# Two 3x3 convolutions on one core: bands of 16 rows on the whole array, or of 8 rows on its quarters

## The chip, the cores and the metric

The kernel runs on one core of a Trainium2 chip. The core has five engines that run side by side and wait for each other through semaphores: TensorE (PE in the profile; its weight loads are PEld), VectorE (DVE), ScalarE (ACT), GpSimd (POOL) and SyncE (SP, which only issues transfers here). 16 DMA engines move data between the large memory (HBM) and the on-chip memory (SBUF), which has 128 partitions. Matrix products land in PSUM, a small memory of eight banks of 512 f32 values per partition. The metric is the device time of one execution in microseconds.

## The reference, cut to what matters

The input is 4 images of 8 channels, 512 x 512, f32. Four layers follow each other, each of the form x = x + f(groupnorm(x)), with 4 groups of 2 channels per image:

```python
x = x + _L0_conv_ref(_gn(x), ...)      # a spiking attention block, 512 x 512 matrices
x = x + _L1_conv_ref(_gn(x), w)        # depthwise 13 x 13, reflected edges
x = x + _L2_conv_ref(_gn(x), w2, b2)   # 3 x 3, 8 to 8 channels, x and w rounded to [-127, 127]
x = x + _L3_conv_ref(_gn(x), w3, b3)   # 3 x 3, 8 to 8 channels, f32
```

Layer 2's rounding scale is 127 / max|groupnorm(x)| over all four images, so nothing of layer 2 can start before layer 1 has ended everywhere. Layer 3's group norm of one image needs layer 2 of that whole image.

## The kernel before, in words

One program, written for a scheduler: the source gives the instructions of each engine, the scheduler sets their order per engine by data dependences and by the buffers of each pool, and every engine then runs its own list strictly in that order. A tile pool with `bufs=n` gives a tag n buffers; the next user of a buffer waits for the last reader of it.

*Layer 0* (`layer0`, the first 2,124 us) and the sums for layer 1's norm (`st1`) are not touched.

*Layer 1* (`layer1`): per group of two channels g, channel b and image t, the whole channel is loaded (two transfers on SP's queue, L667), a banded weight `bt` with norm and residual in it is formed on DVE (L675), and for each of four parts eight f32 products (L684) run: 112 partitions in, 64 out, two halves `q` of the image in the two column halves of the array. ACT evicts (L691), DVE takes statistics (`bn_stats`, L694) and, once per channel and image, the maximum and minimum over 2,048 values (L696, L697). The result goes to HBM (`x2d`, L700, ACT's queue). All four groups' layer 1 norms (`group_stats`, L149 to L167) are computed as layer 1 starts.

*Layers 2 and 3* (`layers23`) hold the image in 37 windows: 16 rows x 8 channels = 128 partitions, stepping by 14 rows. A 3 x 3 convolution is three banded products, one per horizontal tap `dx`, with a 128 x 128 weight that holds the vertical taps (`banded`). Within a row the pixels are kept in four phases (every fourth pixel together); `conv` (L810) needs five products per window, since a neighbour in the outer phases lies in another phase. After layer 1 the weights are built (L740, L744), the norm and the scale for the rounding computed (L753 to L794, with an all-reduce over partitions on POOL), and then five rounds run:

```python
for ks in groups:                      # 12 groups of 3 windows, and one of 1
    if t < T: layer2(t, x3, st3, ks)
    if before is not None:
        for k in ks: layer3(t - 1, before[0], m3, r3, k)
if t < T: halos(x3)
```

Per group `layer2` loads three windows (L827, SP), subtracts and scales on DVE (L834), clips on POOL (L838), rounds to bf16 on DVE (L841), runs the products, and per window evicts with the residual on DVE (L848), adds the bias on ACT (L851) and takes statistics (L852). Per window `layer3` norms on DVE (L865), runs f32 products, evicts with bias and residual on DVE in pixel order (L873) and stores (L879, POOL's queue). `halos` (L857 to L860) copies the rows that windows share from window to window, once per image, as two large transfers and a small one on SP's queue. x3 has two whole-image buffers.

Of the kernel before, what the change touches and what calls it, by code (L numbers as in the profile page):

```python
# [33 lines left out]
F32 = mybir.dt.float32  # L34
# [28 lines left out]
W2_ROWS, W2_STEP, W2_N = 16, 14, 37  # L63
W2_START = [W2_STEP * k for k in range(W2_N - 1)] + [N - W2_ROWS]
W2_VALID = [(0, 15)] + [(1, 15)] * (W2_N - 2) + [(9, 16)]
# [5 lines left out]
def shape_constants():  # L71
# [3 lines left out]
    mask2 = np.zeros((W2_ROWS, B, W2_N, 2), np.float32)  # L75
    for k, (a, b) in enumerate(W2_VALID):
        mask2[a:b, :, k] = 1
# [17 lines left out]
    c24 = np.zeros((3, B, 2 * W2_ROWS - 1, B), np.float32)  # L95
    for dy in range(3):
        c24[dy, np.arange(B), W2_ROWS - 2 + dy, np.arange(B)] = 1
# [4 lines left out]
def network(ctx: ExitStack, tc: tile.TileContext, i: dict, out: bass.AP):  # L102
# [74 lines left out]
    hi = late.tile([P, T, B], F32, name="hi")  # L177
    lo = late.tile([P, T, B], F32, name="lo")
    with ExitStack() as s:
        layer1(  # L180
            s, tc, i, x1d, x2d, avg_quarter, group_stats, st1, st2, hi, lo, band1d
        )
    with ExitStack() as s:
        layers23(s, tc, i, x2d, out, ind, mask2, avg, avg_same, group_stats, st2, hi, lo)
# [436 lines left out]
def layer1(s, tc, i, x1d, x2d, avg, group_stats, st1, st2, hi, lo, band1d):  # L621
    nc = tc.nc
    ps_c = s.enter_context(tc.tile_pool(name="ps_c", bufs=4, space=PSUM))
    ps_1 = s.enter_context(tc.tile_pool(name="ps_2", bufs=1, space=PSUM))
# [25 lines left out]
    for g in range(G):  # L650
        m, r = group_stats(
            st1[g].rearrange("p t b c k (h z) -> p t (b c k h) z", z=3), T, PAIR * NC * 4, None,
            avg, ps_1, f"x1_{g}", n_each=D // 4,
        )
        mr = bp.tile([P, T], F32, tag="mr", name=f"mr_{g}")
        nc.vector.tensor_mul(mr, m, r)
        for b in range(g * PAIR, (g + 1) * PAIR):
# [4 lines left out]
            for t in range(T):  # L662
# [16 lines left out]
                for a in range(n_half // N_PS1):  # L679
# [13 lines left out]
                    )  # L693
                    nc.vector.bn_stats(st2[:, t, b, a, :], xo[:, a, :])  # L694
                flat = xo.rearrange("p a n -> p (a n)")
                nc.vector.tensor_reduce(hi[:, t, b : b + 1], flat, AX.X, ALU.max)  # L696
                nc.vector.tensor_reduce(lo[:, t, b : b + 1], flat, AX.X, ALU.min)  # L697
# [11 lines left out]


def layers23(
    s, tc, i, x2d, out, ind, mask2, avg, avg_same, group_stats, st2, hi, lo
):
    nc = tc.nc
    ps_2 = s.enter_context(tc.tile_pool(name="ps_q", bufs=3, space=PSUM))
    ps_3 = s.enter_context(tc.tile_pool(name="ps_r", bufs=3, space=PSUM))
    ps_1 = s.enter_context(tc.tile_pool(name="ps_3", bufs=1, space=PSUM))
    wpool = s.enter_context(tc.tile_pool(name="w2", bufs=1))

    def col(name, n=1):  # L720
        return wpool.tile([P, n], F32, name=name)

    n_taps = 3 * B
    c24 = wpool.tile([n_taps, i["c24"].shape[1]], F32, name="c24")
    nc.scalar.dma_start(c24, i["c24"])
    w2 = wpool.tile([n_taps, n_taps], F32, name="w2t")
    nc.scalar.dma_start(w2, i["w2"])
    w3 = wpool.tile([n_taps, n_taps], F32, name="w3t")
    nc.scalar.dma_start(w3, i["w3"])
    b2, b3 = col("b2"), col("b3")  # L730
    nc.scalar.dma_start(b2, i["b2"])
    nc.scalar.dma_start(b3, i["b3"])

    def banded(w, dtype, name):

        band = wpool.tile([P, 3, P], dtype, name=name)
        ps = ps_1.tile([P, W2_ROWS, n_taps], F32, tag="misc", name=f"ps_{name}")
        for row in range(W2_ROWS):
            at = (W2_ROWS - 1 - row) * B
            nc.tensor.matmul(  # L740
                ps[:, row, :], lhsT=c24[:, at : at + P], rhs=w, start=True, stop=True
            )
        for dx in range(3):
            nc.vector.tensor_copy(  # L744
                band[:, dx, :].rearrange("p (r c) -> p r c", c=B), ps[:, :, dx * B : (dx + 1) * B]
            )
        return band

    band3 = banded(w3, F32, "band3")


    wall = wpool.tile([P, n_taps * n_taps], F32, name="wall")
# [186 lines left out]
```

## Time and profile before

| what | us |
|---|---|
| runs shown | 3325.26, 3325.86, 3328.9; median 3325.86 |
| the profiled execution | 3325.98, of which the span from first to last instruction 3324.2 |
| layer 1, first to last product | 2129.6 to 2583.8 |
| first product of layer 2 | 2622.6 |
| PE busy | 3086.2 (93%) |
| DVE busy | 2433.7 (73%) |
| POOL busy | 886.1 (27%) |
| ACT busy | 368.8 (11%) |

In the profile's lists a row names line, engine, operation, output <- inputs by the program's names, the shapes, a count, then busy time, the mean of one in ns, and the idle time before it with what ended it. An f32 product is recorded as two passes. A row of a table of windows gives a stretch of the span, busy time of PE, PEld, DVE, ACT and POOL with the number of instructions, the clock that PE was granted as a share of full speed, the busy share of the 16 DMA engines and the GB/s moved. The chain lists, in order of time, what each step waited for, back from the last instruction. All times of instructions are from the start of the span.

### The profile page before, as it was taken

Reading aid. Unit: us, or ns where it says so; the run is one execution under the profiler, and the core shown is the slowest. Engines: PE = TensorE matmul, PEld = TensorE weight load, DVE = VectorE, ACT = ScalarE, POOL = GpSimd, SP = SyncE. Lnnn points to the kernel's source line nnn. Section 1 sums busy time; section 2 is a strip of 40 time slices with the busy share of each in tenths; the row PEclk is TensorE's granted clock in tenths of the full one; section 3 lists DMA queues with packets and bytes.
Section 4 is the critical chain, followed back from the end, with each engine's and each line's share of the span. In section 5 each row is a group of like instructions: output and inputs, shape, how many; then the busy total and the mean of one; then the engine's idle time right before and its main releaser. Section 6 shows DMA issues by size and latency. Waiting matters only on the chain. (4 is left out here: it accounts for less than half of the span.)

```text
span 3324.2 us, 35901 instructions
## 1 busy us (share of the span) xinstructions
PE 3086.2 (93%) x13090; PEld 1633.4 (49%) x13090; DVE 2433.7 (73%) x3751; ACT 368.8 (11%) x545; POOL 886.1 (27%) x1874
## 2 busy tenths in 40 slices
PE   8999999999999999999999999899999449696979
PEld 6555555555555555555555555433334325454545
DVE  5997787797797797788688688555555569696955
ACT  1300000000000000000000000021111121111100
POOL 1332341341342242243243233100000113232322
PEclk9999999999999999999999999899999669898989
DMA  4222212222122221221111111588777245454533
GB/s 169 80 83 65 65 65 77 65 65 73 62 64 71 65 67 63 77 65 64 52 46 55 55 43 40 131 213 213 199 204 204 57 96 137 107 136 101 134 80 84
DMA packets 284406, 315.02 MB, mean 95 GB/s; under 512 B 17424, under 2 KB 197784, under 8 KB 283877
## 3 DMA queue, kind: packets, MB, share of 16 engines
q1 hardware_dynamic: 191040, 200.86, 22.8%
q0 software_dynamic: 22128, 68.09, 6.5%
q10 hardware_dynamic: 71061, 43.78, 4.4%
q8 instruction: 102, 1.67, 0.2%
q14 instruction: 75, 0.61, 0.1%
HBM read 204.84 MB, written 103.17 MB: 93 GB/s over the span
## 5 line engine op out<-in xcount | busy, mean ns | idle before, releaser
L398 PE MATMUL ps_in<-w_v,xn 128*128 128x512 f32 x1024 | 460.1, 598 | 2.5 <-issue 2.2
L810 PE MATMUL ps_conv<-xn,band 128*128 128x128 f32 (+2 forms) x1480 | 415.9, 439 | 46.6 <-DVE xn L865 46.6
L684 PE MATMUL ps_conv<-x,bt 112*64 112x512 f32 x2048 | 448.6, 595 | 4.6 <-issue 3.4
L398 PE MATMUL ps_in<-w_k,xn 128*128 128x512 f32 x1024 | 450.3, 593 | 1.0 <-DVE v_k L363 0.7
L398 PE MATMUL ps_in<-xn,w_q 128*128 128x512 f32 x1024 | 449.6, 592 | 0.2
L434 PE MATMUL ps_b<-toep,vtok 128*64 128x512 bf16 x3072 | 371.8, 382 | 0.0
L810 PEld LDWEIGHTS ps_conv<-xn,band 128*128 128x128 f32 x1480 | 246.5, 196 | 210.0 <-issue 89.0
L684 PEld LDWEIGHTS ps_conv<-x,bt 112*64 112x64 f32 x2048 | 175.3, 135 | 274.6 <-issue 273.4
L461 PE MATMUL ps_out<-wp,so 128*128 128x512 f32 x1024 | 309.0, 444 | 0.0
L483 POOL COPY x1s<-x1s 128x2 f32<-128x2 f32 (+1 forms) x1024 | 226.2, 274 | 297.1 <-DVE x1s L472 297.1
L398 PEld LDWEIGHTS ps_in<-w_k,xn 128*128 128x128 f32 x1024 | 194.1, 190 | 222.4 <-issue 206.2
L398 PEld LDWEIGHTS ps_in<-xn,w_q 128*128 128x128 f32 x1024 | 191.9, 190 | 219.9 <-issue 213.3
L371 POOL TENSOR_TENSOR h_v<-h_v,c_v 128x512 f32<-128x512 f32 x96 | 122.9, 1281 | 656.5 <-DVE h_v L370 622.0
L398 PEld LDWEIGHTS ps_in<-w_v,xn 128*128 128x128 f32 x1024 | 190.3, 190 | 219.1 <-issue 213.6
L434 PEld LDWEIGHTS <-vtok 128*64 128x64 bf16 x3072 | 209.3, 111 | 124.3 <-issue 3.8
L873 DVE SCALAR_TENSOR_TENSOR o<-ps_conv,b,x 128x512 f32<-128x512 f32 x148 | 167.6, 1140 | 123.7 <-PE ps_conv L810 74.5
L346 ACT ACTIVATE h_q<-v_q,c_half 128x512 f32<-128x512 f32 x96 | 69.3, 722 | 1542.6 <-DVE v_q L342 1542.6
L461 PEld LDWEIGHTS ps_out<-wp,so 128*128 128x128 f32 x1024 | 192.7, 188 | 94.1 <-issue 59.0
L167 POOL TENSOR_TENSOR grstd_x<-grstd_x,neg_half 128x1 f32<-128x1 f32 (+2 forms) x25 | 19.4, 775 | 811.3 <-DVE grstd_x L166 679.7
L472 DVE SCALAR_TENSOR_TENSOR x1s<-v_p,xr 128x256 f32<-128x256 f32 x256 | 186.0, 766 | 17.5 <-DMA x<-x1s 5.9
L694 DVE BATCH_NORM_STATS2 st<-xo 128x6 f32<-128x512 f32 x128 | 88.5, 691 | 148.1 <-ACT xo L691 148.1
L810 PE MATMUL ps_conv<-xq,band 128*128 128x128 bf16 (+2 forms) x740 | 119.5, 318 | 68.6 <-DVE xq L841 67.4
(149 smaller groups left out, 3483.9 us busy)
## 6 DMA issues: line engine op xcount, KB each, us to landing
x<-x SPq DMA_DIRECT2D x64, 917.0 KB
x<-x SPq DMA_DIRECT2D x148, 256.0 KB
x<-x1s POOLq DMA_DIRECT2D x128, 262.0 KB, 2.5
x<-in_x SPq DMA_DIRECT2D x128, 256.0 KB
xr<-in_x SPq DMA_DIRECT2D x128, 256.0 KB
x<-xo ACTq DMA_DIRECT2D x64, 512.0 KB
out<-o POOLq DMA_DIRECT2D x140, 224.0 KB, 2.9
xs<-in_x SPq DMA_DIRECT2D x112, 256.0 KB
```

Source lines behind the costliest of these rows:

```text
L167: nc.gpsimd.tensor_tensor(r, r, neg_half[:, :n_groups], op=ALU.pow)
L346: nc.scalar.activation(h, v, AF.Identity, bias=c_col, scale=0.5)
L371: nc.gpsimd.tensor_add(h, h, c_twice[n])
L398: mm = nc.tensor.matmul(ps, lhsT=lhsT, rhs=rhs, start=k == 0, stop=k == NC - 1)
L434: nc.tensor.matmul(pb[two * DH : (two + 1) * DH, :], lhsT=v[:, c, h * DH : (h + 1) * DH], rhs=toep[z][:, h, u : u + N], start=c == 0 and z ...
L461: nc.tensor.matmul(ps, lhsT=so[:, k, c * P : (c + 1) * P], rhs=wpT[z][:, k, :], start=k == 0 and z == 0, stop=k == NC - 1 and z == 1,)
L472: nc.vector.scalar_tensor_tensor(own, v.rearrange("p (g v) -> p g v", g=PH)[:, two, :], 1.0, by_phase[:, two, :], op0=ALU.is_ge, op1=ALU.add,)
L483: nc.gpsimd.tensor_copy(x1[:, f, u : u + n], x1[:, fm, um - n + 1 : um + 1][:, ::-1])
L684: nc.tensor.matmul(ps[q * M1 : (q + 1) * M1, :], lhsT=bt[:, z, :], rhs=xt[:, w0 : w0 + N_PS1, z : z + NV], start=z == 0, stop=z == SHIFTS - 1,
L694: nc.vector.bn_stats(st2[:, t, b, a, :], xo[:, a, :])
L810: nc.tensor.matmul(ps[:, at * NV : (at + n) * NV], lhsT=band[:, dx, :], rhs=x[:, g : g + n, v : v + NV], start=dx == 1, stop=(dx, n) == (2 ...
L873: nc.vector.scalar_tensor_tensor(o.rearrange("p (v g) -> p g v", g=PH), ps.rearrange("p (g v) -> p g v", g=PH), b3, x3[:, k, :].rearrange( ...
```

## The change

Windows of layers 2 and 3 become 8 rows x 8 channels = 64 partitions, stepping by 6 rows: 85 per image, of which numbers k and k + 43 share a tile's two partition halves. A weight is 64 x 64, once per half, and a product uses a quarter of the array. In layer 2 the two halves' products go to the same halves of one PSUM bank. In layer 3 a pair of tiles is taken together, and the second tile's halves are crossed, so that the four quarters each have a product. Two extra phases at the ends of each row (`outer_phases`, copies on POOL) make each tap one product of 512 columns: three per window in place of five.

Layer 3's norm and residual go into its weights (`norm3`: band * r + identity) and its constant into a bias, so x3 is read by PE as it is, and the eviction moves to ACT, which also issues the stores. Layer 2's bias moves into the statistics. Subtract and scale move from DVE to POOL, the clip goes. x3 becomes a ring of 48 tiles (one image has 43, taken as 22 pairs), with `halos` issued every five pairs. The weights are built before layer 1 (`weights23`), layer 2's statistics per group within layer 1, and the all-reduce becomes a transpose and a product.

```diff
-W2_ROWS, W2_STEP, W2_N = 16, 14, 37
+W2_ROWS = 16
+W_IN, W_STEP, W_ALL = 8, 6, 85
+W2_N = 43
+HALF = P // 2
+N_SLOTS = 48
+def window(a, k):
+    q = a * W2_N + k
+    return q * W_STEP, 0 if q == 0 else 1, W_IN if q == W_ALL - 1 else W_IN - 1
+def halves(k):
+    return range(2 if W2_N + k < W_ALL else 1)
...
     with ExitStack() as s:
+        ps_1 = s.enter_context(tc.tile_pool(name="ps_2", bufs=1, space=PSUM))
+        w23 = weights23(tc, i, late, early["y"], ps_1, ident)
         layer1(
...
                     nc.vector.bn_stats(st2[:, t, b, a, :], xo[:, a, :])
-                flat = xo.rearrange("p a n -> p (a n)")
-                nc.vector.tensor_reduce(hi[:, t, b : b + 1], flat, AX.X, ALU.max)
-                nc.vector.tensor_reduce(lo[:, t, b : b + 1], flat, AX.X, ALU.min)
+                    nc.vector.tensor_reduce(hi[:, t, at, a : a + 1], xo[:, a, :], AX.X, ALU.max)
+                    nc.vector.tensor_reduce(lo[:, t, at, a : a + 1], xo[:, a, :], AX.X, ALU.min)
...
+        m, r = group_stats(          # at the end of each group of layer 1
+            st2[:, :, g * PAIR : (g + 1) * PAIR].rearrange("p t b k (h z) -> p t (b k h) z", z=3),
+            T, PAIR * n_a * 2, None, avg, ps_1, f"x2_{g}",
+        )
...
+    def layer2(t, p):
+        ks = [k for k in (2 * p, 2 * p + 1) if k < W2_N]
+        n, n_p = len(ks), HALF * len(halves(ks[-1]))
+        xt = early["x"].tile([P, 2, D], F32, tag="x", name=f"x2_{t}_{p}")
         for j, k in enumerate(ks):
+            for a in halves(k):
+                nc.sync.dma_start(
+                    xt[a * HALF : (a + 1) * HALF, j, :],
+                    bass.AP(
+                        src.tensor, src.offset + window(a, k)[0] * D, [[D, W_IN], [N * D, B], [1, D]]
+                    ),
+                )
+        nc.gpsimd.tensor_scalar(
+            y[:n_p, :n, :], xt[:n_p, :n, :], w["m"][:n_p, t : t + 1], w["r"][:n_p, t : t + 1],
+            op0=ALU.subtract, op1=ALU.mult,
+        )
...
+        outer_phases(xq)
...
+            for dx in range(3):
+                for a in halves(k):
+                    half = slice(a * HALF, (a + 1) * HALF)
+                    mm = nc.tensor.matmul(
+                        ps[half, :], lhsT=w["band2"][half, dx, :], rhs=xq[half, j, dx : dx + PH, :],
+                        start=dx == 0, stop=dx == 2,
+                    )
...
+            nc.vector.bn_stats(st3[:n_p, k, :], own)
+        outer_phases(x3[:n_p, s0 : s0 + n])
...
+    def move(t, a, row, k, to_a, to_row, to_k, n):
+        while n > 0:
+            s0, s1 = slot(t, k), slot(t, to_k)
+            now = min(n, N_SLOTS - s0, N_SLOTS - s1)
+            p0, p1 = a * HALF + row * B, to_a * HALF + to_row * B
+            nc.sync.dma_start(flat[p1 : p1 + B, s1 : s1 + now, :], flat[p0 : p0 + B, s0 : s0 + now, :])
+            n, k, to_k = n - now, k + now, to_k + now
+    def halos(t, k0, k1):
+        for a in range(2):
+            first, n = max(k0, 1), min(k1, W_ALL - a * W2_N) - max(k0, 1)
+            move(t, a, W_STEP, first - 1, a, 0, first, n)
+            move(t, a, 1, first, a, W_IN - 1, first - 1, n)
+        if k1 == W2_N:
+            move(t, 0, W_STEP, W2_N - 1, 1, 0, 0, 1)
+            move(t, 1, 1, 0, 0, W_IN - 1, W2_N - 1, 1)
...
+        for dx in range(3):                        # layer3
+            for j, k in enumerate(ks):
+                for a in halves(k):
+                    half = slice(a * HALF, (a + 1) * HALF)
+                    at = (a ^ j) * HALF
+                    nc.tensor.matmul(
+                        ps[j][at : at + HALF, :], lhsT=band[half, dx, :],
+                        rhs=x3[half, s0 + j, dx : dx + PH, :],
+                        start=dx == 0, stop=dx == 2,
+                    )
+        for j, k in enumerate(ks):
+            o = early["o"].tile([P, D], F32, tag="o", name="o3")
+            nc.scalar.activation(
+                o[:n_p].rearrange("p (v g) -> p v g", g=PH),
+                ps[j][:n_p].rearrange("p (g v) -> p v g", g=PH), AF.Identity, bias=const[:n_p],
+            )
+            for a in halves(k):
+                row, r0, r1 = window(a, k)
+                at = (a ^ j) * HALF
+                nc.scalar.dma_start(
+                    out[t, :, row + r0 : row + r1, :].rearrange("c r w -> r c w"),
+                    o[at + r0 * B : at + r1 * B, :],
+                )
+    chunk = 5
     for t in range(T + 1):
+        if t > 0:
+            norm = norm3(t - 1)
+        for p in range(n_pairs):
             if t < T:
+                did = layer2(t, p)
+                if p % chunk == chunk - 1 or p == n_pairs - 1:
+                    halos(t, p // chunk * 2 * chunk, min(2 * p + 2, W2_N))
+            if t > 0:
+                with tc.issue_after(did):
+                    layer3(t - 1, p, *norm)
```

## The prediction

> **What bounds the kernel now.** I read the slices of the page first, then a table of windows by stage, then the waits, the chain and the DMA issues of the last stage.
>
> ```profile
> PE   8999999999999999999999999899999449696979
> DMA  4222212222122221221111111588777245454533
> ```
>
> Forty slices of 83 us. Layer 0 fills TensorE (PE) to slice 25 and layer 1 to slice 31. The change lies in what follows, and in layer 1's edges. The table of windows, cut at the stages (columns: us, busy PE, weight loads, DVE, ACT, POOL, granted clock, DMA share, GB/s):
>
> ```profile
> 2129.50:2583.80 454.30, 450.21 (x2058) 176.75 (x2058) 241.69 (x251) 87.26 (x127) 3.03 (x3) 0.99 0.80 206
> 2583.80:2622.60 38.80, 15.20 (x68) 14.80 (x68) 13.52 (x38) 0.69 (x1) 4.73 (x3) 0.55 0.15 36
> 2622.60:2724.00 101.40, 40.88 (x190) 20.79 (x191) 73.38 (x108) 25.56 (x37) 18.96 (x26) 0.69 0.41 95
> 2724.00:2887.00 163.00, 129.47 (x558) 77.41 (x558) 126.30 (x181) 25.20 (x37) 50.15 (x100) 0.91 0.51 125
> 3214.00:3324.20 110.20, 98.81 (x372) 60.00 (x372) 56.13 (x75) 0.00 (x0) 24.95 (x72) 0.95 0.29 78
> ```
>
> Layer 1 takes 454 us with PE busy 450; the step to layer 2 38.8 us with PE mostly idle; layer 2 of the first image alone 101 us; each of three mixed rounds (layer 2 of one image, layer 3 of the one before) 163 us; layer 3 of the last image 110 us. In a mixed round PE and DVE are both busy some 127 us. What fills the rest stands in the chain and the waits:
>
> ```profile
> 2710.12 22.97 DMA x<-x
> ```
>
> ```profile
> 2861.32 22.99 DMA out<-o
> ```
>
> ```profile
> DVE o L873 <- DMA out<-o: 49.2, 3, 17.0
> ```
>
> ```profile
> x<-x SPq DMA_DIRECT2D x148, 256.0 KB
> out<-o POOLq DMA_DIRECT2D x140, 224.0 KB, 2.9
> x<-x SPq DMA_DIRECT2D x8, 560.0 KB
> ```
>
> Two edge-row copies of 560 KB, from on-chip memory to itself, end every image. They hold the chain 23 us (50 GB/s), and stores of finished rows, normally landed in 2.9 us, wait behind them for up to 17 us though they come from another queue. The packet records say why: eight packets of 35,840 B are in flight at a time, 4.9 us each, and each copy ends in eight semaphore writes. Its outermost dimension is 8 partitions. The 16-row window loads end in sixteen writes, and a constant load of 24 rows in twelve. So the outer dimension decides how many of the 16 DMA engines carry a copy, and an edge-row copy blocks eight of them for whatever else they are to carry.
>
> **The change, part by part.** The sum is made against the profiled execution (3325.98 us, span 3324.2); the median of the runs is 3325.86, the same.
>
> *DMA.* Every load now has 8 rows outermost (64 partitions), every store 6 (a few 7), every edge copy 8 partitions. By the rows above loads run on 8 engines and stores on 6; I take it that they are the same low-numbered ones, since the edge copies and the stores already collide. Work of one such engine per image:
> - loads: 85 windows x 64 rows / 8 = 680 packets of 2,048 B. In the window of loads just before 2708 us a packet takes 0.127 us, in layer 0's loads 0.084. The addresses are those of the former: 86 us (57 to 86).
> - edge copies: the bands overlap more. 84 neighbours in two directions are 168 copies of 8 x 3,072 B = 4.13 MB, against 1.12 MB before; per engine 516 KB. At 4.9 us per 35,840 B 70 us; at the fastest packet (3.2 us) 46; by the chain's 23 us per 1.12 MB 85. I take 72.
> - stores: 4,096 rows / 6 = 683 packets. A 4,096 B packet of today's stores takes 0.16 (median) to 0.23 us: 55 to 80, I take 68.
>
> Sum 226 us for a mixed round (158 to 251), 158 for the first image (103 to 171), 68 for the last. In pairs of windows (22 per image) a mixed round costs 10.3 us per pair on these engines.
>
> The Trainium skill, "DMA: Bandwidth & Descriptors", section "Why a DMA increments its semaphore by 16 and not by 1", says that the number of engines is the largest up to 16 that divides the slowest dimension of both sides, and that queues of SP and ACT take the lowest-numbered ones; it agrees with the counts 8, 12 and 16 here and speaks against this change. By it the sum is the one above; without it, with 16 engines for loads and stores, it would be the second rival's.
>
> *The compute engines*, per pair: DVE rounds 128x1024 (0.42 for 512, 0.96 for 1536 elements: 0.69) and keeps two evictions (0.739) and two statistics (0.680): 3.5 us. It loses the two 1.14 us evictions, the 0.56 us norms and the 1.08 us subtraction. POOL takes the subtraction (0.61 to 1.48: 1.04) and gains four shifted copies of 254 elements, by the same slope 0.39 each, and a small one: 2.8 us; it loses the out DMAs (0.655 each). ACT gains two evictions in phase order (0.69 contiguous in layer 1, 1.14 for the strided one of DVE today) and four DMA issues (0.58 to 0.68, in layer 1), which stand between the evictions in its order: 3.8 to 4.9, I take 4.2. SP issues four loads of 0.6 and 1.3 edge copies of 0.75: 3.4. PE: layer 1 runs two half-array f32 passes at a time at 448.6/2048 = 0.219 us each; 24 passes for layer 3 are 2.6 us if four run at once, 5.3 if two; layer 2's 12 bf16 products 1.45 (371.8/3072 in layer 0): 4.1 or 6.7. All of it lies beside the DMA's 10.3; if the DMA cover goes, ACT's 4.2 decides and PE's 4.1 is next.
>
> The Trainium skill, "TensorEngine Tiling (Array Packing)", "Gotcha 1: PSUM Pressure", says that different row tiles cannot write one bank at a time. No run here shows row tiles. By that rule PE would pay the two-at-a-time price, which also stays under the DMA.
>
> *Between images* the layer 3 norm and the last edge copies stand before the first layer 3 product: last eviction and statistics 1.4, POOL's edges 0.8, ten copies issued by SP (0.75 each) 7.5, landing 2: 12 us, in place of 23. The ring lets layer 2 run ahead by two pairs only (some 6 us of it).
>
> *Layer 1's start.* The weights of layers 2 and 3 are built before its first product: 64 recorded passes in place of 32 at 7.0 us each, in a row on PE behind their DMAs. The start at 2129.6 can move by nothing, if they fit into the idle 11 us before it, up to 16. I take +12.
>
> *Layer 1's groups.* PE's order now holds the layer 2 statistics of a group, then the layer 1 statistics of the next, then its convolutions; before, all of layer 1's came first. At three borders PE waits: eviction 0.69, statistics and two reduces 2.0, then two chains of reduce, product, variance, product, power and bands like the one before layer 1 (4.8 us), the first longer by five small operations: 13.3, and 2 more for the halved clock (0.50 to 0.55 in idle stretches). 3 x 15 = +45 (27 to 54). The eight reduces of 512 in place of two of 2048 add some 0.6 us on DVE, which is busy 242 of 454.
>
> *Step to layer 2.* Weights are ready, the cross-partition maximum goes through PE: 15 us by the rows of the same small operations, in place of 38.8: -24 (-18 to -28).
>
> Sum:
>
> | | now | then | |
> |---|---|---|---|
> | layer 1 start, groups | | | +57 |
> | step to layer 2 | 38.8 | 15 | -24 |
> | first image | 101 | 158 + 12 | +69 |
> | three mixed rounds | 490 | 3 x (226 + 6) | +206 |
> | last image, ACT 22 x 4.2 | 110 | 95 | -15 |
>
> +293: 3619 us, taken as 3615.
>
> **The rivals.**
> 1. *All 16 engines, edge copies hidden* (the other side). If edge copies overlap other packets on their engine and loads and stores spread, ACT, PE and DVE decide: some 4.7 us per pair with the 0.9 that a mixed round reaches today, 105 per mixed round and 82 for the first image. 57 - 24 + (94 - 101) + (3 x 117 - 490) - 15 = -128: 3198. For it: evictions off DVE, and 23 us stalls gone. Against it: the stores stuck behind edge copies. It decides once a mixed round's DMA falls below about 147 us per engine.
> 2. *Loads and stores on 16, edge copies on 8.* 72 + 43 + 34 = 149 per mixed round, 115 for the first: 57 - 24 + 26 - 25 - 15 = +19: 3345. The loads' count of 16 speaks for it only if partitions, not rows, decide; their 128 partitions and 16 rows do not tell.
> 3. *The quarter products run one after the other.* 24 x 0.43 + 12 x 0.24 = 13.2 us per pair: mixed rounds 296, the last image 227: +617, 3943. Layer 1's column halves, which start 6 ns apart, speak against it.
>
> **How the numbers follow.** Forecast 0.67, with its own range 3480 to 3720 (DMA terms between their ends); rival 1 0.13; rival 2 0.15, within 50 us of its value; rival 3 0.05. 3320 to 3720 takes in the forecast and the greater part of rival 2 and leaves out rivals 1 and 3. Faster by over 0.2% (6.7 us, about what a measurement of this kernel can tell): rival 1 and a little of 2, 0.15; within it 0.02; slower 0.83.
>
> **What would show it.** Right: the DMA share of mixed rounds stays near one half while DVE's rounding or evictions wait on loads and ACT on its own stores; PE busy falls below 60% there with a clock under 0.9; three idle gaps of 13 to 16 us in layer 1; a round of some 230 us. Wrong: mixed rounds near 110 us with ACT as the fullest engine (rival 1), or PE full at 13 us per pair (rival 3). What would make the prediction wrong is above all a copy of 8 rows outermost that runs on more than 8 engines, and edge copies that need less than 46 us per image.

## The result and the profile after

The changed kernel takes 3633.57 us (median of 3631.77 to 3636.43) against 3326.85 for the kernel before beside it: ratio 1.0922, 95% interval 1.0903 to 1.0941. It is slower, by 307 us; the forecast was 3615. The time agrees better than the reasons do, and most of the experiments go to the reasons.

The view of windows of the changed kernel, cut at layer 1, the step to layer 2, the first image, three mixed rounds (from the first layer 3 product of one image to that of the next) and the last image. Columns: length, then busy time and number of instructions of PE, PEld, DVE, ACT and POOL, the clock granted to PE, DMA share, GB/s.

```profile
2135.40:2621.20 485.80, 459.47 (x2072) 169.15 (x2072) 264.15 (x486) 87.18 (x127) 6.05 (x6) 0.95 0.75 194
2621.20:2640.10 18.90, 2.55 (x13) 1.53 (x10) 6.54 (x32) 0.69 (x1) 9.52 (x5) 0.64 0.27 55
2640.10:2816.70 176.60, 56.38 (x275) 26.87 (x274) 79.33 (x126) 0.00 (x0) 118.30 (x136) 0.60 0.37 79
2816.70:3048.50 231.80, 110.91 (x774) 53.23 (x774) 75.05 (x122) 29.54 (x43) 120.21 (x134) 0.73 0.39 102
3048.50:3286.90 238.40, 111.76 (x774) 53.75 (x774) 75.01 (x122) 29.55 (x43) 120.53 (x134) 0.71 0.39 100
3286.90:3519.30 232.40, 103.64 (x761) 51.61 (x761) 71.54 (x117) 29.54 (x43) 115.67 (x129) 0.73 0.39 99
3519.30:3629.70 110.40, 76.14 (x510) 23.86 (x510) 0.00 (x0) 29.55 (x43) 0.06 (x1) 0.93 0.26 77
```

In a mixed round PE is busy 45 to 48% of the time at a granted clock of 0.71 to 0.73, and the share of the 16 DMA engines is 0.39. No engine is full. POOL, which the forecast had at 2.8 us per pair, is the busiest at 120 us.

Where the 305.5 us between the two profiled spans (3324.2, 3629.7) lie. The stages of layers 2 and 3 are cut in both kernels at the first layer 3 product of an image (from 2723.8 to 3216.1 us before, from 2816.7 to 3519.3 after, for the three mixed rounds):

| stage | before | after | difference |
|---|---|---|---|
| layer 1's first product at | 2129.6 | 2135.4 | +5.8 |
| layer 1, first to last product | 453.6 | 485.8 | +32.2 |
| step to layer 2 | 39.4 | 18.9 | -20.5 |
| first image | 101.2 | 176.7 | +75.5 |
| three mixed rounds | 492.3 | 702.6 | +210.3 |
| last image | 108.1 | 110.4 | +2.3 |

What took DVE's place and POOL's, from the costliest groups of the page after (busy time, mean ns; behind the second bar the idle time in front and what ended it):

```profile
L906 PE MATMUL ps_conv<-xq,band 64*64 64x512 bf16 x1020 | 178.2, 483 | 443.1 <-POOL xq L872 388.6
L889 POOL TENSOR_SCALAR y<-x,m_own,r_own 128x1024 f32<-128x1024 f32 x88 | 326.3, 3708 | 259.0 <-DMA x<-x 245.1
L894 DVE TENSOR_SCALAR xq<-y 128x1024 bf16<-128x1024 f32 x88 | 69.5, 790 | 513.4 <-POOL y L889 513.4
```

Line 889, the subtraction and scaling that moved from DVE to POOL, costs 3.71 us per pair where the forecast had 1.04. DVE's rounding and the layer 2 products wait for it; it waits for loads, 24 times, 245 us in all.

The chain of waits over the second mixed round, summed by line:

```profile
by line: DMA x<-x 20.9%; ACTq L992 17.6%; POOL y L889 16.9%; DMA out<-o 16.2%; PE ps_conv L977 5.8%; ACT o L985 5.5%; issue 5.3%; SPq L882 2.6%; PE ps_conv L906 2.5%; DVE x L911 2.1%; POOL xq L873 1.0%; POOL x L873 0.9%; POOL xq L872 0.9%; 
```

Four things share the chain almost evenly: transfers on chip and loads (both are `x<-x`), ACT's issue of stores, POOL's Y, and landing of stores. No one of them is the bound for the whole round.

What the packets say. Their records give the size, the queue and the time of each; work per engine is the summed time of a kind divided by the number of engines it runs on (8, 8 and 6; the number in flight is 8 for 38% of a mixed round, 6 for 19%, and over 10 for 0.1%). The records don't name the engine. But while any edge packet is in flight, all packets together are at most nine, but for under 1 us of the three rounds: copies on eight, loads on eight and stores on six engines take turns, as the forecast took it. Per mixed round, mean of three:

| us per low-numbered engine | forecast | measured | packet |
|---|---|---|---|
| loads | 86 | 66 | 0.100 us for 2,048 B |
| edge copies, 4.13 MB | 72 | 62 | 3.9 us for 30,720 B |
| stores | 68 | 68 | 0.100 us for 2,048 B |
| sum | 226 | 196 | |
| the rest of the round | 6 | 38 | |

The round agrees (232 forecast, 234 measured) because two errors cancel, which is luck: the DMA work was put 30 us too high and everything that isn't DMA 32 us too low. The Trainium skill's rule for the number of engines ("DMA: Bandwidth & Descriptors", "Why a DMA increments its semaphore by 16 and not by 1") agrees with the counts in flight.

### The profile page after: what moved, and what is told of

Same layout as the page of the kernel before. It is cut to its first block, busy times and chain, and to the rows that moved or that the text cites. A ratio compares the mean times of both kernels' runs of the same rounds, so it can differ in the third digit from the quotient of the medians.

```text
span 3629.7 us, 38574 instructions
## 1 busy us (share of the span) xinstructions
PE 3018.2 (83%) x13961; PEld 1511.9 (42%) x13961; DVE 2244.8 (62%) x3752; ACT 385.8 (11%) x569; POOL 1178.8 (32%) x2010
## 5 line engine op out<-in xcount | busy, mean ns | idle before, releaser
L906 PE MATMUL ps_conv<-xq,band 64*64 64x512 bf16 x1020 | 178.2, 483 | 443.1 <-POOL xq L872 388.6
L889 POOL TENSOR_SCALAR y<-x,m_own,r_own 128x1024 f32<-128x1024 f32 x88 | 326.3, 3708 | 259.0 <-DMA x<-x 245.1
L894 DVE TENSOR_SCALAR xq<-y 128x1024 bf16<-128x1024 f32 x88 | 69.5, 790 | 513.4 <-POOL y L889 513.4
L977 PE MATMUL ps_conv<-x,band_t 64*64 64x512 f32 x2040 | 327.7, 683 | 67.4 <-POOL x L970 36.4
L509 POOL COPY x1s<-x1s 128x1 f32<-128x1 f32 (+1 forms) x1024 | 226.1, 271 | 290.5 <-DVE x1s L498 290.5
L906 PEld LDWEIGHTS <-band 64*64 64x64 bf16 x1020 | 82.8, 129 | 546.6 <-issue 523.7
L183 POOL TENSOR_TENSOR grstd_x<-grstd_x,neg_half 128x1 f32<-128x1 f32 (+1 forms) x28 | 20.7, 738 | 822.7 <-DVE grstd_x L182 822.6
L714 PEld LDWEIGHTS ps_conv<-x,bt 112*64 112x64 f32 x2048 | 163.5, 137 | 294.8 <-issue 292.3
L977 PEld LDWEIGHTS ps_conv<-x,band_t 64*64 64x64 f32 x2040 | 129.6, 155 | 206.0 <-issue 104.3
```

Source lines behind the costliest of these rows:

```text
L509: nc.gpsimd.tensor_copy(x1[:, f, u : u + n], x1[:, fm, um - n + 1 : um + 1][:, ::-1])
L714: nc.tensor.matmul(ps[q * M1 : (q + 1) * M1, :], lhsT=bt[:, z, :], rhs=xt[:, w0 : w0 + N_PS1, z : z + NV], start=z == 0, stop=z == SHIFTS - 1,
L889: nc.gpsimd.tensor_scalar(y[:n_p, :n, :], xt[:n_p, :n, :], w["m"][:n_p, t : t + 1], w["r"][:n_p, t : t + 1], op0=ALU.subtract, op1=ALU.mult,)
L894: nc.vector.tensor_scalar(xq[:, :, 1 : PH + 1, :], y[:n_p, :n, :].rearrange("p n (g v) -> p n g v", g=PH), ROUND, ROUND, op0=ALU.add, op1= ...
L906: mm = nc.tensor.matmul(ps[half, :], lhsT=w["band2"][half, dx, :], rhs=xq[half, j, dx : dx + PH, :], start=dx == 0, stop=dx == 2,)
L977: nc.tensor.matmul(ps[j][at : at + HALF, :], lhsT=band[half, dx, :], rhs=x3[half, s0 + j, dx : dx + PH, :], start=dx == 0, stop=dx == 2,)
```

## The experiments

The theory of the forecast is called D in what was put down ahead of the runs: the low engines carry loads, edge copies and stores in turn and set the round. Its rivals are P (POOL's Y), S (the order of SP's queue) and B (the eight partitions of an edge copy).

The table has for each kernel its time, its first image, the mean of its three mixed rounds, the DMA work per low engine in one of them from the packets, and the difference of the two, in us. The experiments in layers 2 and 3 are read from it.

| kernel | time | first image | mixed round | DMA work | rest |
|---|---|---|---|---|---|
| changed | 3633.6 | 176.7 | 234.2 | 196 | 38 |
| Y on DVE | 3535.0 | 144.3 | 215.5 | 197 | 19 |
| loads on 16 engines | 3638.7 | 184.8 | 226.6 | 169 | 58 |
| both | 3510.5 | 146.0 | 201.5 | 169 | 33 |
| no edge copies | 3354.8 | 152.8 | 150.3 | 127 | 23 |
| loads three pairs ahead | 3634.1 | 181.7 | 234.0 | 197 | 37 |
| ahead, 16 engines, Y on DVE | 3515.6 | 149.8 | 204.3 | 171 | 33 |
| edge copies from POOL's queue | 3524.7 | 178.4 | 200.8 | 182 | 19 |
| 16 engines, Y on DVE, POOL's queue, no borders | 3497.8 | 151.0 | 207.2 | 162 | 45 |

**1. Y on DVE**

```diff
-        nc.gpsimd.tensor_scalar(
+        nc.vector.tensor_scalar(
             y[:n_p, :n, :], xt[:n_p, :n, :], w["m"][:n_p, t : t + 1], w["r"][:n_p, t : t + 1],
             op0=ALU.subtract, op1=ALU.mult,
```

> Normalisation Y on VectorE in place of GpSimd, all else as in the changed kernel. Theory D (the eight low DMA engines carry loads, edge copies and stores one after the other and set the mixed round of some 231 us): GpSimd's 3.7 us per pair lie beside that, the mixed rounds stay within 6 us and the time near 3630 (3605 to 3645). Theory P (GpSimd's Y, 22 x 3.7 = 82 us per image and in front of every pair's products, sets the round): mixed rounds fall by 40 to 80 us each, the first image by 60, time 3320 to 3460.

3534.98 us, ratio 1.0617 (1.0598 to 1.0636): 98.6 us faster than the changed kernel. Both theories miss: D said no change, P said 40 to 80 us per mixed round. A mixed round loses 19 us and the first image 32. The group on DVE:

```profile
L889 DVE TENSOR_SCALAR y<-x,m_own,r_own 128x1024 f32<-128x1024 f32 x81 | 66.5, 821 | 382.3 <-DMA x<-x 377.3 <-DMA out<-o 4.4 <-issue 0.5
```

The same operation takes 0.82 us on DVE, and now it waits for loads 377 us. The DMA work is unchanged at 197 us and a round is only 19 us longer than that: with Y off POOL, the low engines nearly are the bound. POOL's Y was a large part of the 38 us rest.

**2. Loads on 16 engines**

```diff
-                        src.tensor, src.offset + window(a, k)[0] * D, [[D, W_IN], [N * D, B], [1, D]]
+                        src.tensor, src.offset + window(a, k)[0] * B * D, [[D, W_IN * B], [1, D]]
...
                 for q in range(2):
+                    for f in range(PH):
...
-                            dst.tensor, dst.offset + (b * N + q * n_half * W1_OUT) * D,
-                            [[NV, M1], [W1_OUT * D, n_half], [1, NV]],
+                                dst.tensor, dst.offset + (q * n_half * W1_OUT * B + b) * D + f * NV,
+                                [[B * D, W1_OUT], [W1_OUT * B * D, n_half], [1, NV]],
...
-                        xo[q * M1 : (q + 1) * M1, :, :].rearrange(
+                            xo[q * M1 + f : (q + 1) * M1 : PH, :, :].rearrange(
```

> Layer 1's result lies in memory row by row with the channels inside a row, so that a load of a band is 64 rows in a row and not 8 rows by 8 channels; layer 1 stores it in eight DMAs of 16 rows per sample in place of two. Theory D: a band load runs on 16 engines, its share of the low eight falls from 680 x 0.101 = 69 to 34 us per image; mixed rounds 231 to about 196, the first image 177 to about 142: time about 3495 (3450 to 3540). Theory P: GpSimd still needs its 119 us per round and its order, the time stays within 20 us of 3634.

3638.7 us, 1.0937 (1.0918 to 1.0957): no gain, as P said. The loads do spread (16 or more packets are in flight for 4% of a mixed round), and the DMA work falls by 27 us per round, but the rest grows by 20. Layer 1 pays for its eight stores (494.2 us from first to last product, 485.8 before). Removing work from the engines that I had called the bound does not shorten the rounds by what it removes: the plain sum of D falls here. The stores stayed on six engines in every run, so what they would gain from 16 is not shown.

**3. Both together**

The two edits above in one kernel.

> Row-by-row layout of layer 1's result (loads on 16 engines) and Y on VectorE together. Theory D: as with the layout alone, 3495, and some 20 to 60 less because the loads that are now early are no longer used up by GpSimd's 5.4 us per pair: low engines 34 + 66 + 68 = 168 us per mixed round, time 3400 to 3480. Theory P: the same as Y on VectorE alone. If both limits hold together, the two edits give more in one kernel than the sum of each alone.

3510.51 us, 1.0544 (1.0527 to 1.0561), 123 us faster than the changed kernel. With Y off POOL, the spread loads are worth 14 us per mixed round where alone they were worth 8 (23 in all, of which a longer layer 1, step and first image took 21 back). It is the pattern that the expectation gave for two limits that hold together, but less than it asked for (3400 to 3480).

**4. No edge copies**

```diff
-                    halos(t, p // chunk * 2 * chunk, min(2 * p + 2, W2_N))
+                    pass
```

> The edge copies between neighbouring bands are left out, so layer 3 reads unfilled edge rows; everything else is computed. Theory D: some 66 us per image of 8-engine work and the landing wait before layer 3 go; mixed rounds 231 to about 160, the first image 177 to about 130, last image unchanged: time about 3375 (3330 to 3440). Theory P: only the wait before the first layer 3 product goes, 12 us four times: 3585 (3560 to 3610).

3354.83 us, 1.0080 (1.0065 to 1.0095). Rounds of 150 us: 84 less than with the copies, of which 62 are the copies' own engine time and the rest waits that they cause. Of the 307 us that the change costs, 279 go with this one part. What is left lies in layer 1's borders and in the first image (152.8 us against 101.2 before); the mixed rounds are 14 us shorter than before. D's numbers hold (3330 to 3440). The granted clock shows it too:

```profile
2790.50:2945.70 155.20, 104.75 (x774) 50.10 (x775) 74.15 (x121) 29.55 (x43) 122.08 (x133) 0.85 0.38 124
```

Behind the length stands PE's busy time: two thirds of the round at a clock of 0.85, where it was 48% at 0.73. POOL, busy 122 of 155 us, is the fullest engine.

**5. Loads three pairs ahead in the order**

```diff
+    for at in order[:n_ahead]:
+        load2(*at)
...
+                for at in order[t * n_pairs + p + n_ahead :][:1]:
+                    load2(*at)
                 did = layer2(t, p)
```

with `layer2` split into `load2` (the tile and its loads) and the rest.

> Only the place of the loads in the order changes: the loads of a pair of bands are issued three pairs earlier, so that SyncE has them out before it issues edge copies that wait for GpSimd and VectorE; the bytes and the engines that carry them are the same. Theory S (at each end of a chunk of five pairs SyncE's queue stands at the edge copies, the loads behind them start late and the whole chain of a pair runs empty: GpSimd's Y idles 245 us in 24 stalls of 10 us behind loads): mixed rounds 232 to 195 to 205, the first image 177 to about 140, time near 3500 (3460 to 3540). Theory D (the low DMA engines are full but for the 8% in which nothing was in flight): mixed rounds not under 213, time 3560 to 3620.

3634.09 us, 1.0925 (1.0907 to 1.0943): nothing. The reason for trying it, from the timelines of SP's queue and of POOL at the end of a chunk in the changed kernel (start, length, number of issues; in brackets the idle time in front):

```profile
2835.66 12.24 SPq L924 DMA_DIRECT2D x<-x  x7
2847.95 1.43 SPq L882 DMA_DIRECT2D x<-x  x2
2849.50 7.38 SPq L924 DMA_DIRECT2D x<-x  x4
2856.93 13.16 SPq L882 DMA_DIRECT2D x<-x  x14
```

```profile
2865.53 3.78 POOL L889 TENSOR_SCALAR y<-x,m_own,r_own 128x1024 f32<-128x1024 f32 x1 [16.42 <-DMA x<-x]
```

Edge copies (L924) hold SP's queue 12 us and again 7, the loads (L882) go out behind them, and POOL stands 16 us. With the loads ahead:

```profile
3049.78 27.89 SPq L883 DMA_DIRECT2D x<-x  x20
3080.32 29.48 SPq L930 DMA_DIRECT2D x<-x  x12
```

```profile
3119.36 3.78 POOL L895 TENSOR_SCALAR y<-x,m_own,r_own 128x1024 f32<-128x1024 f32 x1 [24.40 <-DMA x<-x]
```

Twelve edge copies in a row now hold the queue 29 us, more than the three pairs of loads ahead can cover, and POOL stands 24 us where it stood 16. Issuing a copy is short (0.6 us); SP's queue waits in between for earlier transfers, its waits for stores (`DMA out<-o`) and for loads or copies being 90 and 62 us at the copies' line. In this stall the buffers were not what the loads waited for: the last eviction that frees one ends at 3094.2 us, and the next load is issued at 3112.95, behind the last copy. So the order alone is not the cause here; the copies' time on the queue is. How far ahead the loads can run is set by the four load buffers, though: the load for a pair three ahead takes the buffer of the pair that has just been evicted. More buffers, which might cover a longer hold, were not tried.

**6. Loads ahead, 16 engines, Y on DVE**

The edits of 1, 2 and 5.

> Loads three pairs ahead, layer 1's result row by row (loads on 16 engines) and Y on VectorE, together. If the late loads, the low DMA engines and GpSimd's Y are all that makes a round long, what is left is 34 + 66 + 68 = 168 us on the low engines: mixed rounds about 175, first image about 120, time near 3400 (3350 to 3440). If it stays near the 3510 of the two edits without the early loads, the order of SyncE's queue is not a cause.

3515.57 us, ratio 1.0565 against the 1.0544 of experiment 3: the loads ahead bring nothing here either, as the second half of the expectation has it. It has the same four buffers.

**7. The price of Y on POOL**

```diff
-            y[:n_p, :n, :], xt[:n_p, :n, :], w["m"][:n_p, t : t + 1], w["r"][:n_p, t : t + 1],
+            y[:n_p, :n, :], xt[:n_p, :n, :], 0.0, 1.0,
```

> The price of GpSimd's Y alone: mean and factor are the constants 0 and 1 in the instruction in place of two columns read for each partition, so the numbers are not normalised and the output is not the reference's. If the per-partition operands make it slow, the instruction falls from 3.78 to about 1.0 us (1.478 us for 1536 elements in the kernel before) and the time goes to about that of Y on VectorE, 3535. If it is the operation on 1024 float32 elements itself or other engines' traffic, it stays at 3.7 us and the time at 3630.

```profile
L889 POOL TENSOR_SCALAR y<-x 128x1024 f32<-128x1024 f32 x80 | 290.4, 3630 | 268.0 <-DMA x<-x 259.1 <-issue 8.7 <-POOL xq L873 0.3
```

3.63 us in place of 3.78: the per-partition operands are not what makes it slow. POOL's clip of the kernel before (minimum and maximum with constants, 128 x 1536, in place) takes 1.478 us. So subtract and multiply on POOL cost 3.5 ns per element and minimum and maximum 0.96. Which part of the difference is the operation and which the separate output tile was not tried. The time is 3613.42 us. Of the 14 us that the profiled span is shorter, 11 are the step to layer 2 (8.3 us in place of 18.9), where Y no longer waits for the statistics; mixed rounds stay at 234.

**8. Layer 1's borders**

```diff
+    m_all, r_all = group_stats(
+        st1.rearrange("p g t b c k (h z) -> p (g t) (b c k h) z", z=3), G * T, PAIR * NC * 4, None,
...
     for g in range(G):
-        m, r = group_stats(
...
+        m, r = m_all[:, g * T : (g + 1) * T], r_all[:, g * T : (g + 1) * T]
...
+                if ended and (b, t) == (g * PAIR, 1):
+                    group_end(*ended)
+        ended = g, hi, lo
+    group_end(*ended)
```

where `group_end` holds what stood behind a group's loop: the statistics and maxima of layer 2's input.

> Layer 1 alone: the statistics of all four groups of its input are made in one chain ahead of its first product, and a group's output statistics after the second sample of the next group in place of the border. The three idle gaps of 11.4 to 11.7 us at the borders should fall to under 4 us each, layers 2 and 3 stay: time 3634 - 25 to 34 = 3600 to 3609. If the gaps only move to the new places, 3630.

3595.59 us, 1.0803 (1.0787 to 1.0819), 38 us less. A border in the timeline of PE in the changed kernel:

```profile
2239.43 12.18 PE L714 MATMUL ps_conv<-x,bt 112*64 112x512 f32 x52
2254.43 0.59 PE L167 MATMUL gps_x<-gsum_x,avg 128*128 128x4 f32 x2 [2.83 <-DVE gsum_x L165]
2256.38 0.59 PE L167 MATMUL gps_x<-gsum_x,avg 128*128 128x4 f32 x2 [1.36 <-DVE gsum_x L165]
2257.23 0.59 PE L167 MATMUL gps_x<-gsum_x,avg_quarter 128*128 128x4 f32 x2 [0.26 <-DVE grstd_x L182]
2260.07 0.59 PE L167 MATMUL gps_x<-gsum_x,avg_quarter 128*128 128x4 f32 x2 [2.25 <-DVE gsum_x L165]
2262.71 7.59 PE L714 MATMUL ps_conv<-x,bt 112*64 112x512 f32 x22 [2.04 <-issue]
```

Two chains of two small products each, every one waiting for DVE: 11.1 us from the end of one convolution to the start of the next (the expectation's figure counts the last product in). With the edit no gap over 2 us is left, layer 1 takes 447.3 us in place of 485.8, and the rest of the kernel stays.

**9. Edge copies from POOL's queue**

```diff
-            nc.sync.dma_start(flat[p1 : p1 + B, s1 : s1 + now, :], flat[p0 : p0 + B, s0 : s0 + now, :])
+            nc.gpsimd.dma_start(flat[p1 : p1 + B, s1 : s1 + now, :], flat[p0 : p0 + B, s0 : s0 + now, :])
```

> The edge copies of the changed kernel are issued by GpSimd in place of SyncE, right behind GpSimd's own copies, so that SyncE's loads wait for none of them and, as the stores of the kernel before show for GpSimd's queue, they may run on 16 engines. GpSimd pays some 0.65 us per issue, 28 per image, 18 us. Theory D (the low eight engines' time): 69 + 68 + 33 = 170 us are left there, mixed rounds 232 to 180 to 200, time 3450 to 3520; in a burst the edge copies move over 90 GB/s. Theory B (eight partitions give and take only some 60 GB/s, whatever the number of engines): in a burst the edge copies still move 50 to 65 GB/s, with longer or more packets in flight; rounds fall only as far as loads and stores get past them, 205 to 225, time 3560 to 3620. Theory S (SyncE's queue): the 10 us stalls of Y behind loads go, GpSimd's wait for loads falls from 245 us to under 80.

3524.72 us, 1.0598 (1.0584 to 1.0613), 109 us faster; mixed rounds 200.8. It does not run as D's numbers assumed: an edge copy still has eight packets in flight (at most nine), and while eight are, another packet is for only 8% of that time. A packet is shorter in the mean, 3.3 us against 3.9. By the mean number of edge packets in flight during its life, itself included, a 30,720 B packet took 3.85 us at about eight (4.09 in the changed kernel), 3.34 at seven (3.98) and 2.3 at five (2.2). Eight at a time move 64 GB/s (60 before the move), within B's 50 to 65 and under D's 90, and the time in which any edge packet is in flight hardly changes, 76 us per round against 79. This speaks for a limit that the packets in flight share; single packets spread widely around these means, and no run isolates it. POOL's wait for loads falls to 178 us, not to the 80 of S:

```profile
POOL y L889 <- DMA x<-x: 178.5, 33, 16.2
```

The longest is 16.2 us, against 26.4 in the changed kernel (245.1 us, 24 waits). By these waits, what the move buys is that loads no longer stand behind copies that wait for POOL and DVE: a round is now 19 us above its DMA work. In the chain of one round ACT's issue of stores is gone from the front:

```profile
by line: DMA x<-x 52.4%; SPq L882 15.4%; POOL y L889 11.0%; DVE x L911 6.7%; issue 6.0%; PE ps_conv L977 1.7%; POOL x L970 1.4%; DMA out<-o 1.3%; DVE st L914 1.3%; PE ps_conv L906 1.2%; POOL xq L872 0.8%; ACT o L985 0.3%; POOL x L872 0.2%; 
```

**10. Four edits together**

Experiments 1, 2, 8 and 9 in one kernel.

> The changed kernel with the four edits that gained something or were meant to: layer 1's result row by row, Y on VectorE, edge copies from GpSimd's queue, no borders in layer 1. By theory D and S together (full low engines, and a chain that runs empty when SyncE stands at the edge copies) the borders give 38, the first image falls to about 135, and a mixed round to what the low engines carry, 45 + 62 + 68 = 175, and some 10 of waits: near 3425 (3395 to 3455). If the three edits of the rounds only replace one another, rounds stay near 200 and the time at 3470 or above. Under 3325 would need rounds of 150.

3497.78 us, 1.0507 (1.0492 to 1.0521): 136 us under the changed kernel, while alone the edits of 1, 8 and 9 are worth 98.6, 38.0 and 108.9, 245 in all. The borders' 38 come through (layer 1 takes 451.6 us with the longer stores), the edits of the rounds more than replace one another: 207 us per mixed round, with DMA work down to 162, where edge copies from POOL's queue alone gave 201 and experiment 3 202. What holds it now is read from the chain of the second mixed round, whose sum by line and one turn are:

```profile
by line: DMA x<-x 60.2%; SPq L896 17.0%; DVE x L925 10.0%; DVE y L903 5.7%; issue 4.2%; DVE st L928 1.8%; PE ps_conv L920 0.6%; DVEq L903 0.4%; DVE xq L908 0.2%; PE ps_const L971 0.2%; DVE band_t L963 0.2%; DVE scaled L967 0.1%; DVEq L925 0
```

```profile
3019.98 0.74 DVE x L925
...
3021.87 0.59 SPq L896
...
3022.51 2.69 DMA x<-x
...
3025.32 0.81 DVE y L903
```

An eviction frees a load buffer (four exist), SP issues the next loads into it, they land 2.7 us after their issue here, Y runs, and only behind it in DVE's order stands the next eviction that frees a buffer. This loop turns once per pair. Its longest landings in the round are these, with one of 20.14 us:

```profile
3052.36 14.28 DMA x<-x
3101.77 20.27 DMA x<-x
```

Right around the start of each, POOL issues four edge copies of 240 KB, and until the load lands the packets in flight are mostly those of the copies, up to eight at a time, with some of the loads' and stores' in between. The copies of five pairs go out in one burst, and a load takes as long as the burst. More load buffers, smaller portions of copies or another order of Y and eviction on DVE were not tried, so the loop is read from the chain and not shown by a run.

**11. Early edge copies in the kernel before**

```diff
-    def halos(x3):
-        nc.sync.dma_start(x3[0:B, 1:last, :], x3[W2_STEP * B : (W2_STEP + 1) * B, 0 : last - 1, :])
-        nc.sync.dma_start(x3[P - B : P, 0 : last - 1, :], x3[B : 2 * B, 1:last, :])
+    def halos(x3, k0, k1):
+        first, to = max(k0, 1), min(k1, last)
+        nc.sync.dma_start(x3[0:B, first:to, :], x3[W2_STEP * B : (W2_STEP + 1) * B, first - 1 : to - 1, :])
+        nc.sync.dma_start(x3[P - B : P, first - 1 : to - 1, :], x3[B : 2 * B, first:to, :])
...
                 layer2(t, x3, st3, ks)
+                if at in (5, 9):
+                    halos(x3, groups[at - 5 if at == 5 else 5][0], groups[at][0])
...
-            halos(x3)
+            halos(x3, groups[9][0], W2_N)
```

> The kernel before with one thing of the change: the edge copies of an image go out in three portions, behind the loads of the group after the one that completes them, in place of one burst at the image's end; bands of 16 rows, norms and evictions stay. If the 23 us burst is worth its time on the path, only the last portion (some 8 of 36 neighbours, about 5 us) is left at each image's end: 4 x 18 us less, time near 3255 (3235 to 3280). If the bytes only move to another place, because stores wait behind them there or VectorE and TensorE (126 and 130 of 164 us) fill the round anyway: 3300 to 3330.

3303.12 us, 0.9930 (0.9917 to 0.9944): faster than the kernel before by 24 us, the second expectation's upper end rather than the first's 72. Mixed rounds fall from 164.1 to 153.3 us, the first image grows by 10. The wait in front of an image's first layer 3 product falls from 21 to 22 us to 12. In a round, without the burst:

```profile
2892.40:3046.10 153.70, 131.83 (x561) 77.29 (x560) 129.79 (x184) 25.39 (x37) 54.55 (x101) 0.92 0.50 126
```

PE is busy 132 of 153.7 us and DVE 130. The burst of 23 us covered only some 10 us that nothing else would have taken. Why the first image is 10 us longer was not followed.

**12. The weights ahead of layer 1, on top of that**

```diff
     with ExitStack() as s:
+        ps_w = s.enter_context(tc.tile_pool(name="ps_w", bufs=1, space=PSUM))
+        w23 = weights23(tc, i, late, s.enter_context(tc.tile_pool(name="wall", bufs=1)), ps_w)
         layer1(
```

`weights23` holds the lines on `c24`, `w2`, `w3`, `sw` and both bands, taken out of `layers23`.

> The kernel before with two things of the change: edge copies in three portions, and the weights of layers 2 and 3 built ahead of layer 1 and not behind it. The step from the last layer 1 product to the first of layer 2, 38.8 us, should fall to 17 to 24 us; layer 1's start moves by 0 to 6 us as in the changed kernel (5.8): 15 to 20 less than the portions alone, near 3286 (3278 to 3295). If the step was set by the statistics and the maximum and not by the weights: 3300 to 3306.

3304.84 us, 0.9925 (0.9912 to 0.9939), the same as the portions alone. The step to layer 2 falls from 39.7 to 29.5 us, and layer 1 starts at 2146.2 in place of 2130.8: the step gains 10 and the start loses 15. Two sets of 32 passes, some 7.0 us each set, stand before layer 1, each with a wait in front (PE's timeline of this kernel):

```profile
2123.02 6.99 PE L736 MATMUL ps_band<-w3t,c 24*128 24x24 f32 x32 [6.90 <-DMA w3t<-in_w]
2132.61 6.99 PE L736 MATMUL ps_band<-w2t,c 24*128 24x24 f32 x32 [2.60 <-DVE w2t L757]
```

The changed kernel saves 20 us in this step and starts only 5.8 later. For the start its own timeline has the reason: its bands are 64 wide and not 128, and its two sets take 1.1 and 1.9 us, 11 us less than here.

```profile
2119.64 1.11 PE L783 MATMUL ps_band<-w3t,c 24*64 24x24 f32 x32 [3.08 <-DMA w3t<-in_w]
2126.80 1.91 PE L783 MATMUL ps_band<-w2t,c 24*64 24x24 f32 x32 [6.05 <-DVE w2t L810]
```

For the step, its statistics by group, of which only the last group's are left, would account for the other 10; that is argued, not shown.

## Why the prediction was right, and where it was not

*Direction and size.* 3615 was forecast with 3320 to 3720, 3633.6 was measured. Three kinds of transfer in turn on the same few engines and the edge copies as the greater part of the loss are shown; that the mixed rounds came out within 2 us is luck, since two errors of 30 us cancel in them. Of the signs that were named, PE under 60% with a clock under 0.9 and a round of some 230 us came; the DMA share is 0.39 and not near one half, layer 1's gaps are 11 us and not 13 to 16, and it is POOL's Y that waits for loads, with DVE's rounding behind it.

*Edge copies, loads and stores on the low engines.* The counts were right: 8 and 6 in flight, in turn. The copies are the greater part of the loss, shown by leaving them out (279 of 307 us). "Sum 226 us for a mixed round" was mis-sized: 196. The loads' packet had been put at 0.127 us, from a busy stretch of the kernel before, and takes 0.100; the edge copies' 72 are 62. (The copies before were 1.16 MB with the third, small one, and not 1.12.)

*"All of it lies beside the DMA's 10.3."* This is the step that failed. The forecast added 6 us to the DMA's work for all else; 38 were there. Y on POOL at 3.71 us and not 1.04 is one reason (experiment 1, 19 us per mixed round), SP's queue with edge copies in front of loads another (experiment 9, 33 us, of which 14 are less DMA work by the packets; with four load buffers, issuing loads three pairs earlier on the same queue gained nothing). The forecast counted SP's issues as 3.4 us per pair and did not ask what each of them waits for, nor what stands behind it in the queue. And the engines' sum does not set the round by itself: taking 27 us off it (experiment 2) left the time where it was.

*Layer 1's groups.* "13.3, and 2 more for the halved clock": the gaps are 11.1, 11.2 and 10.8 us. The mechanism is shown by experiment 8; 45 was 33. How the 4 us too many of each divide between the clock and the chain was not followed.

*Layer 1's start.* +12 was taken from between 0 and 16, with 7.0 us for each set of passes; it is +5.8, and the sets take 1.1 and 1.9 us.

*Step to layer 2.* 15 us forecast, 18.9 measured.

*First image.* 170 forecast, 176.7 measured, again with less DMA work (127 us and not 158) and more waits: without POOL's Y it is 144, without edge copies 153.

*Last image.* "22 x 4.2" gave 95; it is 110, as long as before (108). ACT turns once per tile of two bands in 2.38 us in this stretch:

```profile
3568.43 1.54 ACTq L992 DMA_DIRECT2D out<-o  x2
3570.09 0.69 ACT L985 ACTIVATE o<-ps_conv,const 128x512 f32<-128x512 f32 x1 [1.69 <-issue]
```

Two issues at 0.77 and an eviction of 0.69 make 4.75 per pair with the gaps, 102 us for 43 tiles; the forecast had 0.58 to 0.68 per issue and under 3 us to fill and drain.

*The rivals.* Rival 3 (quarter products one after another) is out: 24 passes of a pair take 3.45 us, and the first sixteen starts in the record come in fours, 6 to 7 ns apart, one four 0.43 to 0.48 us after the other; the last eight come in twos.

```profile
3566.08 3.45 PE L977 MATMUL ps_conv<-x,band_t 64*64 64x512 f32 x24 [1.30 <-ACT o L985]
```

The rule that the forecast weighed from the Trainium skill ("TensorEngine Tiling (Array Packing)", "Gotcha 1: PSUM Pressure") does not show here as a price: the two row halves of a pair write the two halves of one bank in the same four, and the pair stays well under the 5.3 us of two at a time. Rival 1 needed loads and stores on 16 engines and hidden edge copies; rival 2 only the former. Experiment 2 gave the loads their 16 engines and the time did not move; the stores stayed on six. That rival 2's sum would have failed too, for the same reason as the forecast's, is likely and not shown.

## What to carry to other kernels

A copy between partitions costs by its bytes and by its place in a queue: here 4.13 MB per image on eight engines cost 62 us of engine time and 84 us of the round, and with another queue a round was 33 us shorter. When bands are made narrower, count the overlap first: 8 rows with a step of 6 carry 3.55 times the edge bytes of 16 rows with a step of 14, 2.4 times as many row copies and each 1.5 times as long, since the two extra phases travel with them. Copying the four phases alone, a third fewer bytes, was not tried. A sum of work on the fullest resource is a lower bound; for the rest, follow each queue in order and ask what its next instruction waits for. Two edits that each win may win by the same stall; run them together before adding their gains (245 us alone, 136 together, and a mixed round longer than with one of them).

## What the runs showed of the hardware

- Subtract and multiply of 1024 f32 per partition on POOL takes 3.6 to 3.8 us with constants or per-partition operands, 0.82 us on DVE; minimum and maximum of 1536 takes 1.48 on POOL.
- An edge copy of eight partitions runs eight packets at a time from SP's and from POOL's queue. A 30,720 B packet takes 3.3 to 4.4 us in the mean in these kernels, 1.1 us at its fastest, and in the changed kernel 4.1 us with about eight such packets in flight and 2.2 with about five. A limit that they share (theory B) fits that; it was not isolated.
- Four 64 x 64 quarter products of f32 run at once, 0.43 us from one four of 512 columns to the next.
